# The product with V turned round: channels instead of queries on the partitions

## The chip, the core and the metric

The kernel runs on one core of one Trainium2 chip, in float32 throughout. The metric is the device time of one execution in microseconds (us). The core has five engines that work side by side, each through its own list of instructions in order: TensorE (PE in the profile; PEld is its loading of weights, which overlaps the products), VectorE (DVE), ScalarE (ACT), GpSimd (POOL) and SyncE (SP), which here only issues DMAs. TensorE multiplies a stationary operand (the "weights", loaded first) with a moving one and writes to PSUM, whose banks hold 512 float32 numbers on each of 128 partitions. A product whose output needs only 64 or 32 of the partitions can be one of two or four "column tiles", which stand side by side in the array.

## What is computed

For each of 16 samples: x is 100 x 640, the context 722 x 384, of which the last four rows (`ca`) are tokens of their own.

```python
query = x @ Wq                              # 100 x 640
keyt, valt = enc @ Wk, enc @ Wv             # 718 x 640 each
hs = mha(query, keyt, valt)                 # 8 heads of 80 channels, softmax over 718 keys
ca_q1 = einsum('btc,th->bch', ca, Wq_ca)[:, indices]
ca_q2 = mha(ca_q1, x, x) @ Wq
ca_hs2 = mha(ca_q2, ca @ Wk_ca, ca @ Wv_ca) # softmax over only 4 tokens
out = (hs + ca_hs2) @ Wout + b_out + x
```

## The kernel before, in words

Everything runs in one loop over the samples b = 0 to 15, whose instructions are written out in a fixed order for every engine (a manual schedule: no planner moves anything). One pass of the loop holds, in the order of TensorE's list:

- three groups of scores for b (`scores(b, 0..2, ...)`, L615), each two of the six blocks of 119 or 120 keys, copied by ScalarE to three tiles `st` with keys on partitions and 8 x 100 columns of heads and queries;
- the small products of the token attention (`z_ps`, L821, and `y_ps`, L759);
- before the change, the five transposes (`hst_ps`, L936) of the result of b - 1;
- the values of b and the keys of b + 1 in turn (`Values`, `Keys`, L441 and L472), while VectorE and ScalarE turn the scores into exponentials;
- the last chunk of the keys (`kT_ps`, L566), the projection by Wout of rows that are complete (`project`, L964), and in every second pass the queries of the next two samples (`queries`, L542);
- the product of the exponentials with V (`a_ps`, L1326).

PSUM is divided into three pools of two slots: `ps2` (pairs of banks), `psk` and `ps1` (single banks). The pool `ps1` matters here: both halves of the product with V take its two banks, and so do, next, the third and fourth bank of `scores(b + 1, 1)`, then `z_ps` and `y_ps`. A slot can be written again only when the last reader of its former contents is done.

The product before: the exponentials of 64 or 36 queries (`QC`) are the stationary operand, the 80 channels of one head and a column of ones (`vs`, `D + 1`) the moving one. So queries stand on the partitions of the result, and the sum of the exponentials comes out as an 81st column in the same partition. Four heads (`g`) share a bank. VectorE takes the reciprocals of the four sums, multiplies (L1338, L1340), and adds the tokens' second sums `hs2` (L1347). For the projection the result must have channels on partitions, hence the transposes at the start of the next pass, copied by ScalarE (L949) into `hsT`.

The tokens' second sums: `softmax3` (L866 to L869) makes 8 x 4 weights for each query, `load` (L840) brings the four tokens' values by one DMA of 1 MB on POOL's queue, broadcast to 100 partitions, and `values2` multiplies and adds them on POOL (L883, L890). Also on POOL: the first attention's scores of the tokens (`scores1`, L794 and L801), the sums of the context from which products are saved (`enc_sums`, L507), the masked `m2` (`keys`, L731) and the residual's bias (L921).

SP's list holds the loads of the samples to come (`load_enc`, L229, each waiting until the values of b are done; `load_rest`, `ca`, `load_m`) and the stores of `out` (L986).

The product and the division before (L1326 to L1347):

```python
for g in range(2):
    a_ps = psum1(f"a_ps_{b}_{g}")                 # one bank of ps1 for four heads
    ...
            for lo, hi in QC:                     # two column tiles: 64 and 36 queries
                nc.tensor.matmul(
                    a_v[lo:hi, h % 4],
                    st[i // 2][: KEYS[i], i % 2, h * S + lo : h * S + hi],
                    block(i, h // 4)[: KEYS[i], h % 4],   # 80 channels and the ones
    ...
    nc.vector.reciprocal(rs.unsqueeze(2), a_v[:, :, D : D + 1])
    nc.vector.tensor_tensor(hs[:S, cols]..., a_v[:, :, :D], rs..., ALU.mult)
    if b:
        nc.vector.tensor_tensor(hs[:S, cols], hs[:S, cols], hs2[:, cols], ALU.add)
```

## Time and profile before

| | |
|---|---|
| runs, median (lowest to highest) | 951.72 us (951.39 to 953.53), 3 runs |
| the profiled execution: span from first to last instruction | 950.1 us (no time beside the span is given) |
| TensorE busy | 943.5 us, 99% |
| VectorE / POOL / ScalarE busy | 681.0 / 620.7 / 364.6 us |
| TensorE's share of the chain that ended last | 96% |

In the profile a line such as "L1326 PE MATMUL a_ps<-vs,st" is a group of instructions of one line of the program: engine, operation, the tile written and the tiles read, then shapes (partitions x elements), the count, busy time and mean duration in ns, and after the bar the idle time before them with what ended it. In a timeline the first two numbers are the start from the beginning of the span and the length in us; neighbours of one kind are merged with their count, and one merged row runs a little into the next, since matmuls are pipelined. A float32 matmul shows as two instructions. "to landing" is the time from a DMA's issue until its data is there.

### The profile page before, as it was taken

The numbers are of one execution on the slowest core, as the hardware profiler recorded it, in microseconds if no ns is written. First come the engines' busy times: TensorE is split into PE (matmuls) and PEld (weight loads), VectorE is DVE, ScalarE is ACT, GpSimd is POOL, SyncE is SP. The second block draws the span as 40 slices with busy tenths as digits, with TensorE's granted clock in tenths as the row PEclk, the third lists the DMA queues.
The fourth block names the chain that finished last, engine by engine and source line by source line (L and its number), as shares of the span: only waits on it lengthen the run. The fifth ranks groups of instructions, "written<-read, shape, count | busy, mean of one in ns | idle before, by whom it ended". The sixth has DMA issues, their size and how long they took to land.

```text
span 950.1 us, 22551 instructions
## 1 busy us (share of the span) xinstructions
PE 943.5 (99%) x9679; PEld 798.3 (84%) x9679; DVE 681.0 (72%) x1079; ACT 364.6 (38%) x605; POOL 620.7 (65%) x565
## 2 busy tenths in 40 slices
PE   9999999999999999999999999999999999999998
PEld 6988879788897888888788887987889888897866
DVE  3859794977829687595956959578693886939684
ACT  1244443424335244443524334244431434434241
POOL 5757976876738757594872948657694576748514
PEclk9999999999999999999999999999999999999999
DMA  8822023040310404003040120403113030120200
GB/s 259 290 73 79 2 82 113 1 129 2 94 58 1 116 2 134 4 23 108 1 150 3 42 74 1 137 2 96 35 41 111 1 113 4 54 56 1 93 8 29
DMA packets 45355, 62.28 MB, mean 66 GB/s; under 512 B 13448, under 2 KB 37320, under 8 KB 43656
## 3 DMA queue, kind: packets, MB, share of 16 engines
q1 hardware_dynamic: 41720, 42.97, 15.0%
q0 software_dynamic: 2512, 16.72, 6.0%
q8 instruction: 76, 1.25, 0.5%
q10 hardware_dynamic: 1024, 1.15, 0.4%
q14 instruction: 23, 0.19, 0.1%
HBM read 55.26 MB, written 5.57 MB: 64 GB/s over the span
## 4 chain that ended last, share of the span: by engine, by line
PE 96%; DVE 2%; DMA 1%; issue 0%; ACT 0%; POOL 0%; ACTq 0%; DVEq 0%
PE s_ps L615 13%; PE a_ps L1326 12%; PE v_psA L441 10%; PE v_psB L441 8%; PE kT_ps L566 8%; PE k_psA L472 7%; PE q_ps L542 7%; PE o_ps L964 7%; PE k_psB L472 6%; PE v_psC L441 3%; PE k_psC L472 3%; PE v_ps L382 2%; PE y_ps L759 2%; PE v_psD L441 2%; PE v_psE L441 2%; PE k_psE L472 1%
## 5 line engine op out<-in xcount | busy, mean ns | idle before, releaser
L794 POOL TENSOR_TENSOR e<-ca,g 100x800 f32<-100x800 f32 x64 | 100.0, 1572 | 150.3 <-ACT vs L414 146.5
L883 POOL TENSOR_TENSOR hs<-vb,p 100x640 f32<-100x640 f32 x64 | 105.5, 1657 | 46.7 <-DVE p L869 34.2
L890 POOL TENSOR_TENSOR hs<-hs,hs 100x640 f32<-100x640 f32 x48 | 113.9, 2373 | 3.8
L1326 PEld LDWEIGHTS a_ps<-vs,st 120*36 120x36 f32 (+3 forms) x3072 | 109.1, 125 | 5.6 <-issue 5.5
L1326 PE MATMUL a_ps<-vs,st 120*36 120x81 f32 (+3 forms) x3072 | 111.9, 233 | 0.0
L507 POOL TENSOR_TENSOR enc<-enc 128x240 f32<-128x240 f32 x135 | 98.9, 742 | 19.4 <-DMA enc<-in_enct 12.3
L441 PE MATMUL v_psA<-wv_sb,enc 128*120 128x320 f32 x352 | 109.5, 434 | 0.0
L1153 DVE TENSOR_TENSOR st<-st,over 120x1600 f32<-120x1600 f32 x48 | 106.6, 2222 | 0.0
L650 ACT COPY st<-s_ps 120x800 f32<-120x800 f32 x64 | 49.7, 829 | 148.0 <-PE s_ps L615 148.0
L801 POOL TENSOR_TENSOR e<-e,e 100x800 f32<-100x800 f32 x48 | 90.5, 1885 | 3.8
L441 PE MATMUL v_psB<-wv_sb,enc 128*120 128x320 f32 x296 | 91.9, 433 | 0.0
L615 PE MATMUL s_ps<-qp,kT 64*120 64x100 f32 x1536 | 88.5, 268 | 0.0
L615 PEld LDWEIGHTS s_ps<-qp,kT 64*120 64x120 f32 x1536 | 83.1, 182 | 5.6 <-issue 4.2
L1338 DVE RECIPROCAL rs<-a_ps 100x4 f32<-100x4 f32 x32 | 5.8, 182 | 114.2 <-PE a_ps L1326 114.2
L472 PE MATMUL k_psA<-enc,wk_sb 128*128 128x240 f32 x360 | 87.6, 366 | 0.0
L472 PEld LDWEIGHTS k_psA<-enc,wk_sb 128*128 128x128 f32 x360 | 68.3, 190 | 16.7
L1161 ACT ACTIVATE st<-st 120x1600 f32<-120x1600 f32 x48 | 73.9, 1539 | 22.0 <-DVE st L1153 22.0
L441 PEld LDWEIGHTS v_psA<-wv_sb,enc 128*120 128x120 f32 x352 | 63.2, 183 | 22.6 <-issue 0.5
L1165 DVE TENSOR_TENSOR most<-most,st 120x800 f32<-120x800 f32 x64 | 65.9, 1029 | 20.5 <-ACT st L644 19.1
L472 PE MATMUL k_psB<-enc,wk_sb 128*128 128x240 f32 x300 | 73.0, 366 | 0.0
L441 PEld LDWEIGHTS v_psB<-wv_sb,enc 128*120 128x120 f32 x296 | 54.0, 183 | 21.9 <-DVE vs L412 0.4
L542 PE MATMUL q_ps<-xT,wq_sb 128*128 128x200 f32 x400 | 69.1, 333 | 0.0
(146 smaller groups left out, 1728.2 us busy)
## 6 DMA issues: line engine op xcount, KB each, us to landing
vb<-va_d POOLq DMA_DIRECT2D x16, 1000.0 KB, 7.5
enc<-in_enct SPq DMA_DIRECT2D x30, 240.0 KB, 3.8
enc<-in_enct SPq DMA_DIRECT2D x15, 360.0 KB, 3.3
xT<-in_xt SPq DMA_DIRECT2D x8, 500.0 KB, 4.0
rest<-in_enct SPq DMA_DIRECT2D x31, 120.0 KB, 6.3
xn<-in_x SPq DMA_DIRECT2D x11, 320.0 KB, 4.8
out<-xn SPq DMA_DIRECT2D x11, 320.0 KB, 2.5
ca<-in_cas SPq DMA_DIRECT2D x16, 156.2 KB
```

Source lines behind the costliest of these rows:

```text
L441: nc.tensor.matmul(at[0][j][:KN, : H // 2], a_form(self.enc, f)[:, j * KN : (j + 1) * KN], wv_there.get(f, wv_sb[:, W_AT[f]]), start=first ...
L472: nc.tensor.matmul(at[:, i * KT : (i + 1) * KT], wk_sb[:, W_AT[f], i], a_form(self.enc, f), start=(first and i == 0), stop=last, skip_grou ...
L507: nc.gpsimd.tensor_tensor(out, left, right, op)
L542: nc.tensor.matmul(q_ps[:, : 2 * S].rearrange("p (j s) -> p j s", j=2), wq_sb[:, c, n * P : (n + 1) * P], xT[:, :, c, :], start=(c == 0), ...
L566: nc.tensor.matmul(bank[:, i * KT : (i + 1) * KT], weights[c], a_raw(enc, u, c), start=(i == 0 and c == 0), stop=(c == CC - 1), skip_group ...
L615: nc.tensor.matmul(s_ps[bank][:n, 256 * a + lo : 256 * a + lo + rhs.shape[-1]], kT[rows, c, u, j * KN : (j + 1) * KN], rhs, start=bank not ...
L794: first = nc.gpsimd.tensor_tensor(to, self.ca[:, t, :].unsqueeze(1).to_broadcast([S, NH, S]), g[:, :, t].unsqueeze(2).to_broadcast([S, NH, ...
L801: nc.gpsimd.tensor_tensor(e, e, to, ALU.add)
L883: first = nc.gpsimd.tensor_tensor(to, vb[:S, t, :].rearrange("p (h d) -> p h d", h=NH), p2[:, :, t].unsqueeze(2).to_broadcast([S, NH, D]), ...
L890: nc.gpsimd.tensor_tensor(sums, sums, to, ALU.add)
L1153: return nc.vector.tensor_tensor(st[i], st[i], top.over[:KN].unsqueeze(1).to_broadcast([KN, 2, ROWS]), ALU.subtract,)
L1326: nc.tensor.matmul(a_v[lo:hi, h % 4], st[i // 2][: KEYS[i], i % 2, h * S + lo : h * S + hi], block(i, h // 4)[: KEYS[i], h % 4], start=(i ...
```

## The change

The product with V is turned round: the values are the stationary operand and the exponentials of all 100 queries the moving one, so that channels stand on the partitions and queries along the free axis. Each head's 80 channels are split into 64 "wide" and 16 "narrow" ones. The wide ones of two heads fill two column tiles of 64 in one bank (`a_ps`, four pairs of heads by 100 queries). The narrow ones of a head share a column tile of 32 with 16 columns of ones in another bank (`r_ps`, heads 0 to 3 and 4 to 7 beside each other), so that the sums of the exponentials come out on 16 partitions per head. The narrow products of all heads and keys come first, then the wide ones.

The result now stands as the projection needs it, in another order of channels, to which Wout's rows are loaded (`load_outputs`, 16 DMAs for one). The transposes and ScalarE's copies of them go. The division needs each head's reciprocals on the partitions of its channels: `divide` takes the reciprocal of the narrow bank on VectorE, writes one row per head to DRAM (two DMAs), and reads it back broadcast to 16 partitions for each head and to 64 for pairs (eight and two DMAs), all on SP's queue, into the tile `ratio`. Then VectorE multiplies the narrow bank, adds its two halves (the unwanted part is zeroed by `ratio`), multiplies the wide bank (`scale`), and adds the second sums (`place`).

The tokens' second sums are turned too: the tokens' values `vaT` are computed with channels on partitions and stay there, and the softmax weights of each pass are transposed in blocks of 32 by VectorE, written to DRAM in four DMAs and read back broadcast in ten, on SP's queue; POOL's multiplications and additions then have 500 elements on 128 partitions instead of 640 on 100. `softmax3` and `keys` move to earlier places in the pass.

```diff
-QC = [(0, 64), (64, S)]
+REST = 2 * (D - 64)
+SLOT = D + REST // 2
+VALUES = (0, REST // 2)
+ONES = (D, 0)
+WIDE = (0, REST)
+NARROW = (64, 0)
+FIRST = (0, D - 64)
...
+def load_outputs(load, to, w):
+    rows = w.rearrange("(h k) n -> h k n", h=NH)
+    for h in range(NH):
+        g, e = h // 4, h % 2
+        load(out=to[64 * e : 64 * e + 64, h // 2], in_=rows[h, FIRST[g] : FIRST[g] + 64])
+        at = 32 * (h % 4) + 16 * g
+        load(out=to[at : at + 16, HC - 1], in_=rows[h, 64:] if g == 0 else rows[h, : FIRST[1]])
...
-        def load(self):
-            self.vb = vb = vb_tile(f"vb_{b}")
-            nc.gpsimd.dma_start(out=vb[:S],
-                in_=va_d[b * T : (b + 1) * T, :].unsqueeze(0).to_broadcast([S, T, H]))
...
             nc.vector.reciprocal(sm, sm)
             nc.vector.tensor_tensor(
-                p2, e, sm.unsqueeze(2).to_broadcast([S, NH, T]), ALU.mult
+                p2_in[:S].rearrange("p (h t) -> p h t", h=NH), e, ..., ALU.mult
             )
+            turned = small.tile([P, HT], F32, tag="p2t", name=f"p2t_{b}")
+            nc.vector.transpose(turned, p2_in)
+            p2_d = dram.tile([HT, S], F32, tag="p2_d", name=f"p2_d_{b}", bufs=2)
+            for lo, hi in QZ:
+                nc.sync.dma_start(out=p2_d[:, lo:hi], in_=turned[lo : lo + 32, : hi - lo])
+            heads = p2_d.rearrange("(h t) q -> h (t q)", h=NH)
+            for e in range(2):
+                nc.sync.dma_start(out=self.pb[64 * e : 64 * e + 64, : HC - 1],
+                    in_=heads[e::2].unsqueeze(0).to_broadcast([64, HC - 1, T * S]))
+            for h in range(NH):
+                at = 32 * (h % 4) + 16 * (h // 4)
+                nc.sync.dma_start(out=self.pb[at : at + 16, HC - 1],
+                    in_=heads[h].unsqueeze(0).to_broadcast([16, T * S]))
...
-        def transpose(self, chunks=[(0, HC)], get=psumk):
...
+        def divide(self, rests):
+            b = self.b
+            inverse = small.tile([P, 2, S], F32, tag="inv", name=f"inv_{b}")
+            nc.vector.reciprocal(inverse, rests)
+            inv_d = dram.tile([NH, S], F32, tag="inv_d", name=f"inv_d_{b}", bufs=2)
+            for g in range(2):
+                nc.sync.dma_start(
+                    out=inv_d[4 * g : 4 * g + 4], in_=inverse[16 * (1 - g) :: 32, g])
+            for h in range(NH):
+                at = 32 * (h % 4) + 16 * (h // 4)
+                nc.sync.dma_start(out=ratio[at : at + 16, HC - 1 + h // 4],
+                    in_=inv_d[h].unsqueeze(0).to_broadcast([16, S]))
+            for e in range(2):
+                nc.sync.dma_start(out=ratio[64 * e : 64 * e + 64, : HC - 1],
+                    in_=inv_d[e::2].unsqueeze(0).to_broadcast([64, HC - 1, S]))
+            self.parted = inverse
+            nc.vector.tensor_tensor(inverse, rests, ratio[:, HC - 1 :], ALU.mult)
+
+        def scale(self, wides):
+            for to, cols in self.pieces():
+                nc.vector.tensor_tensor(
+                    to[:, HC - 1], self.parted[:, 0, cols], self.parted[:, 1, cols], ALU.add)
+            for to, cols in self.pieces():
+                nc.vector.tensor_tensor(
+                    to[:, : HC - 1], wides[:, :, cols], ratio[:, : HC - 1, cols], ALU.mult)
+
+        def place(self):
+            for to, cols in self.pieces():
+                nc.vector.tensor_tensor(to, to, self.hs2[:, :, cols], ALU.add)
...
-                for lo, hi in QC:
-                    nc.tensor.matmul(
-                        a_v[lo:hi, h % 4],
-                        st[i // 2][: KEYS[i], i % 2, h * S + lo : h * S + hi],
-                        block(i, h // 4)[: KEYS[i], h % 4],
...
+        rests = psum1(f"r_ps_{b}")[:, : 2 * S].rearrange("p (g q) -> p g q", g=2)
+        for i in range(len(KC)):
+            for g in range(2):
+                for j in range(4):
+                    h = 4 * g + j
+                    nc.tensor.matmul(
+                        rests[32 * j : 32 * j + 32, g],
+                        slot(i, h)[:, NARROW[g] : NARROW[g] + REST],
+                        st[i // 2][: KEYS[i], i % 2, h * S : (h + 1) * S],
...
+        wides = psum1(f"a_ps_{b}")[:, : 4 * S].rearrange("p (c q) -> p c q", c=4)
+        for i in range(len(KC)):
+            for h in range(NH):
+                lo = WIDE[h // 4]
+                nc.tensor.matmul(
+                    wides[64 * (h % 2) : 64 * (h % 2) + 64, h // 2],
+                    slot(i, h)[:, lo : lo + 64],
+                    st[i // 2][: KEYS[i], i % 2, h * S : (h + 1) * S],
...
+        mine.divide(rests)
+        mine.scale(wides)
+        mine.hs2 = now.hs2
+        if b:
+            mine.place()
```

(`pieces` gives the parts of a sample's 100 rows that fall into one block of 128 output rows: one or two, for b = 14 three.)

More of the change, by code (lines that the diff above doesn't have):

```diff
@@ new lines, in pieces @@
+        def pieces(self):
+            b = self.b
+            for r, (lo, n) in enumerate(OC):
+                first, end = max(lo, b * S), min(lo + n, (b + 1) * S)
+                if first >= end:
+                    continue
+                if r not in hsTs:
+                    hsTs[r] = (
+                        spare[0].rearrange("p (c s) -> p c s", c=HC)
+                        if r == len(OC) - 1
+                        else hsT_tile(f"hsT_{r}")
+                    )
+                yield hsTs[r][:, :, first - lo : end - lo], slice(first - b * S, end - b * S)
@@ L1171 @@
             enc_sums(enc)
-            now.load()
             now.softmax1()
@@ L1263 @@
                     nc.scalar.copy(wv_sb[:, W_AT[f]], wv_there.pop(f))
-            second.load()
             if b == 1:
```

233 lines of the change are left out of this document (112 added, 121 removed).

## The prediction

> **What bounds the kernel now.** I read the totals and the chain that ended last first, then the timelines of one steady pass (b = 9, which begins its product with V at 551.28 us), then the DMA rows. The totals and the chain, from the page:
>
> ```profile
> span 950.1 us, 22551 instructions
> PE 943.5 (99%) x9679; PEld 798.3 (84%) x9679; DVE 681.0 (72%) x1079; ACT 364.6 (38%) x605; POOL 620.7 (65%) x565
> PE 96%; DVE 2%; DMA 1%; issue 0%; ACT 0%; POOL 0%; ACTq 0%; DVEq 0%
> ```
>
> TensorE never stands still for long: a microsecond off its own work is a microsecond off the span, and any wait put into its queue is added in full. The other engines have slack. TensorE's timeline around the product (start, duration):
>
> ```profile
> 551.28 6.99 PE L1326 MATMUL a_ps<-vs,st 120*64 120x81 f32 x192
> 558.20 1.93 PE L615 MATMUL s_ps<-qp,kT 64*120 64x100 f32 x32
> ...
> 566.03 0.75 PE L821 MATMUL z_ps<-y,e 100*32 100x33 f32 x64
> 566.71 1.21 PE L759 MATMUL y_ps<-m,xT 128*100 128x96 f32 x10
> 567.75 0.59 PE L936 MATMUL hst_ps<-ident,hs 100*128 100x100 f32 x5
> 568.18 1.26 PE L441 MATMUL v_psA<-wv_sb,enc 128*120 128x320 f32 x4
> ```
>
> Start to start, the product takes 6.92 us, the three groups of scores 7.83 us (558.20 to 566.03, 2.61 each), the transposes of the result 0.43 us (567.75 to 568.18).
>
> **TensorE's own work.** Before, 192 instructions run as pairs of column tiles: 96 pairs of 81 columns, 72 ns a pair, or 0.89 ns a column. After, the wide part has 96 instructions in 48 pairs of 100 columns, the narrow part 96 instructions in 24 fours of 100 columns. At 0.89 ns a column that is 4.27 and 2.14 us. Four column tiles do run side by side: the z row has 64 instructions in 0.68 us, 42.5 ns per four with 33 columns, which is 13 ns above 0.89 a column; with that surcharge the fours cost 2.45. I take 4.35 + 2.25 = 6.6 us, a gain of 0.3 (bounds 0.5 and 0). The five transposes go: 0.43. Over 15 passes: 15 x 0.73 = 11.0 us less; the last pass is summed apart. The other way to write the tokens' values at the start (60 small matmuls for 12) is within a microsecond, and I leave it out.
>
> **The new wait.** Before, a sum is finished on VectorE as soon as its half of the product is there (start, duration, idle before):
>
> ```profile
> 551.45 0.82 DVE L983 TENSOR_TENSOR xn<-o_ps,xn 128x640 f32<-128x640 f32 x1 [0.77 <-PE o_ps L964]
> 554.95 0.18 DVE L1338 RECIPROCAL rs<-a_ps 100x4 f32<-100x4 f32 x1 [2.67 <-PE a_ps L1326]
> 555.16 0.49 DVE L1340 TENSOR_TENSOR hs<-a_ps,rs 100x320 f32<-100x320 f32 x1
> ...
> 558.33 0.18 DVE L1338 RECIPROCAL rs<-a_ps 100x4 f32<-100x4 f32 x1 [1.74 <-PE a_ps L1326]
> 558.54 0.49 DVE L1340 TENSOR_TENSOR hs<-a_ps,rs 100x320 f32<-100x320 f32 x1
> ```
>
> Its two banks are free at 559.03, and the next user of those two banks, the second group of scores, gets to them at 558.20 + 2.61 = 560.8. With channels on partitions the sums of the exponentials lie along the free axis of a few partitions and must be spread over the others. `divide` does that through DRAM: reciprocal, two writes, eight narrow and two wide broadcast reads, all on SP's queue, and VectorE waits in order. Both banks (`r_ps`, `a_ps`) are held until the last product is out, and they are the very two that `scores(b + 1, 1)` takes. In the compiled order, TensorE's third and fourth instruction of that group wait for VectorE. So I time the chain against TensorE, from the product's start.
>
> The rows for its steps: two reciprocals of different width, the issue of a store and of a broadcast load on SP (minimum, median, maximum in ns), and the time to landing (the last column):
>
> ```profile
> L1338 DVE RECIPROCAL rs<-a_ps 100x4 f32<-100x4 f32 x32 | 5.8, 182 | 114.2 <-PE a_ps L1326 114.2
> L830 DVE RECIPROCAL rz<-z_ps 100x8 f32<-100x8 f32 x16 | 3.2, 200 | 0.0
> L1061 SPq DMA_DIRECT2D m_d<-m x5: 319/328/413, 27.1 to 31.1; - x5
> L749 SPq DMA_DIRECT2D ca<-in_cas x15: 314/393/509, 30.3 to 781.7; - x15
> out<-xn SPq DMA_DIRECT2D x11, 320.0 KB, 2.5
> enc<-in_enct SPq DMA_DIRECT2D x4, 60.0 KB, 3.2
> GB/s 0 178 325 213 227 293 179 87 261 79 11 0 0 11 0 0 0 11 0 0 0 0 0 0 0 0 0 0 0 0 11 0 0 0 0 0 0 0 217 347
> ```
>
> 1. The narrow sums end at 2.25; VectorE, free since 552.27, starts at 2.4.
> 2. The reciprocal is now 128x200. Four more elements cost 18 ns, 4.5 each, so 182 + 196 x 4.5 = 1.06 us: 3.5. (Lower bound, if width costs what it costs L1340, (491 - 182) / 316 = 0.98 each: 0.37 us.)
> 3. Two writes at 0.33 each, begun at 3.6 and 3.9. Landing: the 320 KB store took 2.5 us. The last row is the traffic from 541 to 600 us in 40 slices of 1.48; the store ran in the ninth, at 261 GB/s, so without its bytes it would take 1.25. For 1.6 KB I take 2.2, nearer the upper end, because the 60 KB load took 3.2 although it is smaller: the first lands at 5.8, the second at 6.1. In the tenth slice (554.3 to 555.8) the traffic ends, so nothing stands ahead.
> 4. Ten reads at 0.39 (the broadcast load of `ca`) begin at 5.85; the eighth starts at 8.6, the tenth at 9.4. A read lands after 1.25 to 3.2 us (the store's floor, the smallest load, which had other loads beside it); I take 2.4: 11.0 and 11.8.
> 5. VectorE: `rests` times the ratio, 200 from PSUM, by L1340's slope 0.37; one or two adds of 0.2; `wides` times the ratio, 400 from PSUM, 0.57, or 0.75 in two pieces. The add fits before the last landing; so 11.8 + 0.7 = 12.5, and TensorE hears at 12.6.
>
> TensorE itself is there at 6.6 + 2.6 + 0.1 = 9.3. The wait is 3.3 us, and 15 x 3.3 = 49.5 (bounds below). Queued behind it on TensorE is everything. On VectorE the running maximum (562.68 before, 11.4 after the start of the product) waits behind the chain and then the added second sums, to about 13.4; but its second step waits for TensorE's stalled scores anyway, so I count no second wait.
>
> [...]
>
> **The end.** Today's last pass:
>
> ```profile
> 932.87 6.14 PE L1326 MATMUL a_ps<-vs,st 120*64 120x81 f32 x168
> 939.26 1.06 PE L1326 MATMUL a_ps<-vs,st 120*64 120x81 f32 x24
> 941.98 4.50 PE L964 MATMUL o_ps<-wout_sb,spare 128*128 128x320 f32 x16
> 946.51 0.49 DVE L977 TENSOR_TENSOR spare<-o_ps,spare 128x320 f32<-128x320 f32 x1 [1.12 <-PE o_ps L964]
> ```
>
> From 932.9 to 950.1 it takes 17.2 us. After: ratio landed at 11.8, product 0.6 and second sums 0.7 on VectorE, 20 projection matmuls at 4.50 / 16 = 0.27, 5.4, then 0.5 and a store of 0.35 + 2.5: 21.9. That is 4.7 more.
>
> **The tokens' second sums.** The 1 MB load on POOL's queue, known long ahead, becomes four writes and ten broadcast reads on SP's, behind the softmax. What hides it:
>
> ```profile
> 578.43 1.00 DVE L715 STREAM_TRANSPOSE over<-spread 128x800 f32<-128x800 f32 x1
> 580.63 1.88 POOL L801 TENSOR_TENSOR e<-e,e 100x800 f32<-100x800 f32 x1
> 584.79 4.01 POOL L883 TENSOR_TENSOR hs<-vb,p 100x640 f32<-100x640 f32 x2 [2.28 <-DVE p L869]
> 596.31 3.01 POOL L890 TENSOR_TENSOR hs<-hs,hs 100x640 f32<-100x640 f32 x1
> vb<-va_d POOLq DMA_DIRECT2D x16, 1000.0 KB, 7.5
> ```
>
> The weights are now made just ahead of `over`, by 579.3. Four issues (1.3), a landing (2.2) and 7.5 for the megabyte give 590.5; POOL, free at 582.5 and then busy about 3 with the residual's bias and the moved `keys`, waits some 5 us. Its seven steps took 14.5 us (584.79 to 599.32); with 500 elements instead of 640 about 11.4, ending at 602, 2.6 later than before. `place` wants them one pass on, near 620, and the enc sums that follow on POOL wait for loads issued only at 595.9. So nothing. If 18 us of cover were gone, VectorE would stand in `place`, after the banks are free. SP's queue, held to about 585 by these, is free again before the loads of 595.9. VectorE's added work (reciprocal, 0.4 for the turned weights) lies in its idle time; ScalarE only loses the result copies.
>
> **The first pass.** There SP's queue is not empty:
>
> ```profile
> 83.36 0.42 DVE L869 TENSOR_TENSOR p<-e,sm 100x32 f32<-100x32 f32 x1
> 84.55 0.94 SPq L242 DMA_DIRECT2D rest<-in_enct  x2
> 92.41 6.98 PE L1326 MATMUL a_ps<-vs,st 120*64 120x81 f32 x192
> ```
>
> Before, SP had issued everything for pass 0 by 86. Now Wout (16 issues instead of one), the queries' input and the loads of b = 2 stand behind the turned weights of 83.8: their writes have landed at 87.3, and 33 issues (10 + 16 + 7) of 0.39 last to 100.2, with 4.3 MB, 12.4 us at 347 GB/s. The reciprocal's writes, wanted at 92.4 + 3.6 = 96.0, leave 4.2 us late and share the engines with what is in flight; I take 6 more for this pass (bounds 0 and 12).
>
> **The sum.** 950.1 - 11.0 + 49.5 + 6.0 + 4.7 = 999.3 us of span. The page gives no time of the profiled execution beside its span; the median of the runs, 951.72, stands 1.6 above it, which I add: **1001 us**.
>
> **The rivals.** (a) The round trip hides and the change is faster. The chain must be 3.3 us shorter: reciprocal 0.37 (0.7 less), landings at 1.25 both (2.1), issues at 0.31 (0.7), together 3.5. Then the steady waits are gone and the end costs 1.2; with the first pass at 2, 950.1 - 11.0 + 2 + 1.2 = 942.3, and 944 us. With my end and first pass it wins only under a steady wait of (11.0 - 4.7 - 6.0) / 15 = 0.02 us. Each shortening is possible, all three together hardly: 0.08. Between 949.8 and 953.6 (0.2%, about what these times can tell from no change): 0.02.
>
> (b) TensorE restarts slowly after each wait. The first rows of the timeline:
>
> ```profile
> 1.13 2.50 PE L1014 MATMUL idle_ps<-idle 128*128 128x128 f32 x10 [1.13 <-DVE idle L1011]
> ...
> 4.84 2.25 PE L382 MATMUL v_ps<-wv_sb,enc 128*120 128x320 f32 x4
> ...
> 9.42 1.24 PE L382 MATMUL v_ps<-wv_sb,enc 128*120 128x320 f32 x4
> ```
>
> From rest, 128 columns took 250 ns, where 0.89 a column makes 114, and four v_ps took 2.25 us instead of 1.24 later (with load waits in it). The slow stretch lasted from 1.13 to 3.63 or 7.09, 2.5 to 6 us, and half of it was lost. If a wait of 3.3 us does the same, each loses 1.25 to 3 us more; at 1.7, 15 x 1.7 = 25, 1026 us. [...] No steady pass here has a gap to show it. 0.13.
>
> (c) The reads are slow: issues at 0.51 (the row's maximum) and landings of 2.5 and 3.2 add 2.3 us: 16 x 2.3 = 37, 1038 us. 0.10.
>
> (d) Column tiles of 32 do not run four abreast: 96 x 89 ns makes the product 12.8 us and 90 us more; the z row speaks against it. 0.01.
>
> **How the numbers follow.** My own case, a steady wait of 1.3 to 5 us, holds 0.66: 1001 - 30 = 971 to 1001 + 26 = 1027. To hold 8 in 10 I go from 966 to 1036, which takes in (b) and most of (c) and leaves out (a), (d) and the far tails. Faster by over 0.2%: 0.08; within: 0.02; slower: 0.90.
>
> **What would show it.** The waits should list the second group of scores behind VectorE's product with `ratio`, 15 times at 3 to 4 us; SP's rows ten ratio reads a pass at 0.3 to 0.4; the reciprocal near 1.06 us; product instructions at 4.3 and 2.2 us a pass; no hst_ps rows. A TensorE without that wait would prove me wrong.

## The result, and the profile after

| | before | after |
|---|---|---|
| runs, median (lowest to highest) | 951.92 us (951.39 to 953.53), 4 runs | 1103.54 us (1102.45 to 1107.45), 4 runs |
| ratio, 95% interval | | 1.160 (1.158 to 1.162) |
| the profiled execution | span 950.1 us | 1107.45 us, span 1105.7 us |

The change costs 152 us. The forecast, 1001 us (966 to 1036), had the direction and the main place of the loss, and a third of its size.

The page of the changed kernel: totals, the granted clock by slices, and the chain that ended last.

```profile
span 1105.7 us, 23133 instructions
PE 1000.2 (90%) x9647; PEld 837.1 (76%) x9647; DVE 689.3 (62%) x1116; ACT 356.7 (32%) x578; POOL 552.8 (50%) x554
PEclk9899599898998989899998989989899998989898
PE 60%; DVE 19%; DMA 9%; SPq 8%; issue 3%; ACT 0%; DVEq 0%; POOL 0%
```

TensorE now stands still for a tenth of the span, and although it has less to do than before its busy time rose from 943.5 to 1000.2 us: part of its work runs at a lower clock (0.931 of full in the mean of the span, 0.999 before). The round trip of the reciprocals (DVE, DMA, SPq) has come into the chain. Around one steady product, the one of b = 8 by the count of starts (the one at 551.28 us before, which the prediction called b = 9), TensorE's timeline, start and duration first:

```profile
642.11 2.27 PE L1382 MATMUL r_ps<-st,vs 120*32 120x100 f32 x96
644.32 4.34 PE L1394 MATMUL a_ps<-st,vs 120*64 120x100 f32 x96
648.59 1.93 PE L647 MATMUL s_ps<-qp,kT 64*120 64x100 f32 x32
650.45 1.28 PE L647 MATMUL s_ps<-qz,kT 32*120 32x200 f32 x20
653.21 0.57 PE L647 MATMUL s_ps<-qz,kT 32*120 32x200 f32 x2 [1.48 <-DVE inv L993]
656.11 1.66 PE L647 MATMUL s_ps<-qz,kT 32*120 32x200 f32 x10 [2.34 <-DVE hsT L1015]
657.69 5.63 PE L647 MATMUL s_ps<-qp,kT 64*120 64x100 f32 x64
```

The product is 6.48 us from start to start (6.92 before). Then come two waits for the two banks, 1.48 and 2.34 us, and behind them 64 score instructions take 5.63 us for which 3.60 were enough before:

```profile
561.62 3.60 PE L615 MATMUL s_ps<-qp,kT 64*120 64x100 f32 x64
```

The changed kernel's stretch by windows (length; busy time and count of PE, PEld, DVE, ACT and POOL; PEclk, DMA share, GB/s):

```profile
651.60:655.20 3.60, 0.69 (x4) 0.28 (x2) 0.70 (x3) 1.44 (x2) 0.00 (x0) 1.00 0.43 83
655.20:662.00 6.80, 5.89 (x52) 5.43 (x54) 2.29 (x5) 1.24 (x3) 0.00 (x0) 0.50 0.02 4
662.00:664.20 2.20, 2.20 (x48) 1.86 (x48) 1.60 (x2) 0.53 (x2) 0.00 (x0) 1.00 0.00 0
```

The granted clock falls to 0.50 at 655.2, near the end of the second wait, and is back at full at 662.0, 6.8 us later. The other steady stretches are alike: the clock is low for 6.8 us in ten of the fourteen and for 10.2 us in four. VectorE's timeline and then SP's show the chain, and last stand the rows of the read issues (minimum, median, maximum in ns):

```profile
644.46 1.41 DVE L975 RECIPROCAL inv<-r_ps 128x200 f32<-128x200 f32 x1 [1.34 <-PE r_ps L1382]
652.69 0.36 DVE L993 TENSOR_TENSOR inv<-r_ps,ratio 128x200 f32<-128x200 f32 x1 [6.83 <-DMA ratio<-inv_d]
655.32 0.64 DVE L1015 TENSOR_TENSOR hsT<-a_ps,ratio 128x384 f32<-128x384 f32 x2 [1.90 <-DMA ratio<-inv_d]
```

```profile
645.89 1.13 SPq L978 DMA_DIRECT2D inv_d<-inv  x2
647.58 3.85 SPq L983 DMA_DIRECT2D ratio<-inv_d  x8
651.47 1.30 SPq L988 DMA_DIRECT2D ratio<-inv_d  x2
```

```profile
L983 SPq DMA_DIRECT2D ratio<-inv_d x128: 302/418/1877, 125.1 to 1088.8; - x128
L988 SPq DMA_DIRECT2D ratio<-inv_d x32: 608/629/1268, 128.7 to 1090.0; - x32
```

The waits of the whole span (total, times, longest):

```profile
PE s_ps L647 <- DVE inv L993: 45.6, 15, 16.3
PE s_ps L647 <- DVE hsT L1015: 26.0, 13, 2.4
PE y_ps L791 <- POOL m L763: 9.8, 1, 9.8
PE o_ps L1033 <- DVE spare L1021: 8.8, 1, 8.8
...
ACT beside L1165 <- DMA wvca<-in_wvca: 17.5, 1, 17.5
...
POOL ratio L1197 <- DMA m_d<-ratio: 9.5, 1, 9.5
```

Cut at the starts of the 16 products, each span falls into four parts: the start (up to the first product), the first stretch (to the product of b = 1), the 14 stretches that follow (the "passes 1 to 14" of the expectations), and the end (from the last product's start). The table holds them for every kernel, from TensorE's timelines; the runs are told below.

| us | start | first stretch | 14 stretches (each against before) | end | span | median of the runs |
|---|---|---|---|---|---|---|
| before | 92.4 | 58.3 | 782.2 | 17.2 | 950.1 | 951.9 |
| after | 104.5 | 81.8 | 892.9 (+7.9) | 26.5 | 1105.7 | 1103.5 |
| e1_no_trip | 104.2 | 62.3 | 776.9 (-0.4) | 18.4 | 961.8 | 964.5 |
| e2_dummies | 101.5 | 81.3 | 890.5 (+7.7) | 25.4 | 1098.6 | 1102.2 |
| e2b_four_dummies | 102.6 | 81.3 | 849.1 (+4.8) | 26.0 | 1059.0 | 1061.8 |
| e3_startup | 101.1 | 83.0 | 891.2 (+7.8) | 26.0 | 1101.4 | 1101.3 |
| e3b_memset_later | 100.6 | 82.4 | 887.0 (+7.5) | 26.0 | 1096.0 | 1099.9 |
| e4_wout_first | 101.9 | 70.8 | 889.4 (+7.7) | 26.1 | 1088.2 | 1091.1 |
| e5_scalar_empties | 103.1 | 77.2 | 820.4 (+2.7) | 25.5 | 1026.2 | 1026.8 |
| v1_pool_scales | 93.0 | 59.2 | 784.5 (+0.2) | 26.6 | 963.3 | 965.1 |
| e6_start_and_wout | 92.5 | 71.5 | 890.2 (+7.7) | 26.0 | 1080.2 | 1080.8 |
| v3_picked_end | 92.7 | 60.6 | 784.5 (+0.2) | 19.0 | 956.8 | 959.1 |
| v4_softmax_back | 92.9 | 60.1 | 774.7 (-0.5) | 19.1 | 946.8 | 948.2 |
| e7_two_queues | 101.0 | 80.6 | 879.6 (+7.0) | 25.4 | 1086.5 | 1088.6 |

So the 155.6 us of span are 12.1 at the start, 23.5 in the first stretch, 110.7 in the fourteen, and 9.3 at the end. The first of these moves by 3 to 4 us between kernels that do not touch it (101.0 to 104.5); less than that is not read from it.

### The profile page after: what moved, and what is told of

Read it like the earlier page. It is cut to its first block, busy times and chain, and to the rows that moved or that the text cites. A ratio compares the mean times of both kernels' runs of the same rounds, so it can differ in the third digit from the quotient of the medians.

```text
span 1105.7 us, 23133 instructions
## 1 busy us (share of the span) xinstructions
PE 1000.2 (90%) x9647; PEld 837.1 (76%) x9647; DVE 689.3 (62%) x1116; ACT 356.7 (32%) x578; POOL 552.8 (50%) x554
## 3 DMA queue, kind: packets, MB, share of 16 engines
q8 instruction: 76, 1.25, 0.5%
## 4 chain that ended last, share of the span: by engine, by line
PE 60%; DVE 19%; DMA 9%; SPq 8%; issue 3%; ACT 0%; DVEq 0%; POOL 0%
PE s_ps L647 12%; PE kT_ps L598 6%; PE q_ps L574 6%; PE o_ps L1033 6%; SPq L983 6%; DMA ratio<-inv_d 4%; PE v_psB L473 4%; PE v_psA L473 4%; PE k_psA L504 3%; PE k_psB L504 3%; PE r_ps L1382 3%; PE v_psC L473 3%; DVE most L1241 3%; DMA inv_d<-inv 3%; DVE vs L444 2%
## 5 line engine op out<-in xcount | busy, mean ns | idle before, releaser
L647 PE MATMUL s_ps<-qz,kT 32*120 32x200 f32 x768 | 70.4, 398 | 76.0 <-DVE inv L993 45.6
L929 POOL TENSOR_TENSOR hs<-pb,vaT 128x500 f32<-128x500 f32 x64 | 79.9, 1259 | 113.2 <-DMA pb<-p_d 92.2
L647 PEld LDWEIGHTS s_ps<-qp,kT 64*120 64x120 f32 x1536 | 117.1, 244 | 9.5 <-issue 7.7
L647 PE MATMUL s_ps<-qp,kT 64*120 64x100 f32 x1536 | 122.5, 332 | 0.0
L539 POOL TENSOR_TENSOR enc<-enc 128x240 f32<-128x240 f32 x135 | 101.2, 759 | 37.0 <-DMA enc<-in_enct 29.7
L647 PEld LDWEIGHTS s_ps<-qz,kT 32*120 32x120 f32 x768 | 47.3, 201 | 88.6 <-issue 76.2
L1229 DVE TENSOR_TENSOR st<-st,over 120x1600 f32<-120x1600 f32 x48 | 96.0, 2002 | 0.0
L993 DVE TENSOR_TENSOR inv<-r_ps,ratio 128x200 f32<-128x200 f32 x16 | 5.9, 366 | 129.7 <-DMA ratio<-inv_d 129.7
L676 ACT COPY st<-s_ps 120x400 f32<-120x400 f32 x64 | 28.3, 499 | 135.4 <-PE s_ps L647 135.4
L1394 PE MATMUL a_ps<-st,vs 120*64 120x100 f32 (+1 forms) x1536 | 69.5, 250 | 0.0
```

What stands on the lines that cost most here:

```text
L539: nc.gpsimd.tensor_tensor(out, left, right, op)
L647: nc.tensor.matmul(s_ps[bank][:n, 256 * a + lo : 256 * a + lo + rhs.shape[-1]], kT[rows, c, u, j * KN : (j + 1) * KN], rhs, start=bank not ...
L929: first = nc.gpsimd.tensor_tensor(to, pb[:, :, t], va.to_broadcast([P, HC, S]), ALU.mult)
L1229: return nc.vector.tensor_tensor(st[i], st[i], top.over[:KN].unsqueeze(1).to_broadcast([KN, 2, ROWS]), ALU.subtract,)
L1394: nc.tensor.matmul(wides[64 * (h % 2) : 64 * (h % 2) + 64, h // 2], slot(i, h)[:, lo : lo + 64], st[i // 2][: KEYS[i], i % 2, h * S : (h + ...
```

## The experiments

**Without the round trip** (e1_no_trip). The two writes and ten reads of `divide` are taken out, so the kernel leaves the division undone.

> The changed kernel without the round trip: the reciprocal is still taken, but its two writes to DRAM and the ten reads into `ratio` are left out, so the sums are multiplied by whatever `ratio` holds and the division is left out of the result. Theory 1 (the second scores wait for the two banks until the round trip is over, and TensorE's clock then falls for some microseconds): both go with the trip. Per pass 1 to 14 the changed kernel is 7.9 us behind the kernel before; with the trip gone it should be 0.9 us ahead of it (product -0.44, transposes -0.43). Pass 0 loses its 18.3 us of wait and about 4 us of slow clock, and ends within 1 us of before's. The end loses its 8.8 us wait and about 2.3 us of slow clock. The start-up keeps its +12.1. Sum: 950 + 12 - 13 + 1 - 2 = 948 of span, so about 950 us by the clock of the runs; the bounds are 943 and 956. Rival (what is slow is something the change does beside the trip: narrow tiles, the turned second sums on GpSimd, VectorE's larger product): the time stays above 1000 us, and the passes stay several us longer than before's although TensorE's wait for `inv` is gone.

Measured: 964.5 us, ratio to before 1.013 (1.011 to 1.016). The fourteen stretches fall from +7.9 to -0.4, so the trip carries the steady loss and the turned products and sums none. That is half of the 0.87 a stretch that the product and the transposes save. Most of the rest goes at one place, where k_psE waits for VectorE to empty the V bank: in the stretch of b = 8 everything ahead of it keeps the 0.87, and what stands behind it has lost 0.45 to 0.49 us of that, though the list of waits has only 0.22 there. The time is 14 us above the 950 expected, and outside its bounds: 13 were subtracted for the fourteen stretches where 5.3 came, the first stretch is at +4.0 and not +1, the end at +1.2 and not -2. What is left without the trip is 11.8 at the start, 4.0 in the first stretch and 1.2 at the end; the division is not the whole loss. In the first stretch TensorE's timeline has a wait for the queries' input, whose load stood behind Wout's:

```profile
121.45 1.29 PE L791 MATMUL y_ps<-m,xT 128*100 128x96 f32 x10 [1.94 <-DMA xT<-in_xt]
122.53 2.38 PE L473 MATMUL v_psA<-wv_there,enc 128*120 128x320 f32 x4
```

Four instructions take 2.38 us after that one wait, not the 1.26 of the prediction's row; the granted clock was 0.50 from 122.5 to 124.7 us.

**Keeping TensorE at work during the wait** (e2_dummies, then e2b_four_dummies).

```diff
+        if g == 1 and b:
+            for _ in range(9):           # e2b: 4
+                nc.tensor.matmul(s_ps[0], ident, wq_sb[:, :4, :P], start=True, stop=True, ...)
         for part, last in zip((rests, halves) if g == 1 else ...
```

> The changed kernel with nine more matmuls of 128x128 by 128x512 in each pass but the first, just ahead of the second scores group, into its first bank, which the scores then open anew, so that nobody reads them. They take about 0.43 us each (a 320-column matmul takes 0.27 to 0.28 us from start to start), 3.9 us in all, and need nothing of the round trip: they fill the gap of 1.5 + 2.3 us in which TensorE waits for the two banks. The wait is not shortened by it, TensorE is only kept at work. Theory 1a (after the gap the clock has fallen to about half and is back only some 6 us later, which costs 3.5 to 4 us in every pass): granted clock in the second scores back to 0.9 and more, scores after the gap in 4.4 to 5.2 us and not 8.0, so each of 15 passes is 3.5 us shorter and the time falls to about 1053 us (1045 to 1062) although each pass has more work. Rival 1b (the scores after the gap are slow for a reason of their own, such as the banks, their operands or traffic on the ports): more work, nothing gained, 1103 us or up to 1110. Rival 1c (the matmuls do not fit into the gap): up to 59 us slower, 1160 us.

Measured: 1102.2 us, the same as without them. That decides nothing, since the matmuls were twice as long as assumed: a float32 matmul is two instructions, 18 of 0.444 us are 8.0 us a stretch. But e1's stretches plus 8.0 are -0.4 + 8.0 = +7.6, and +7.7 was measured, with the granted clock at 0.988 over the span. So in the steady stretches the waits for the banks and the slowness had gone, and just the dummies' own time had come. Four of them fit the gap:

> As the run with nine extra matmuls, but with four. In that run each extra matmul of 512 columns turned out to be two instructions of 0.444 us, so nine took 8.0 us and not 3.9; its passes were all alike (62.09, 65.17, 70.55 us), which is what the kernel without the round trip takes plus 8.0, with no wait left and the clock at 0.99. Four take 3.55 us, just under the gap of 1.5 + 2.3. Theory 1a (the clock falls in the gap, and its return costs 3.5 to 4 us in each pass): a pass is that without the trip (54.0, 57.0, 62.4) plus about 3.8 of gap or dummies, 57.8 instead of 62.3, so 14 passes gain about 4.4 each and the time falls to about 1042 us (1033 to 1055). Rival 1b (the scores after the gap are slow for a reason of their own, not because TensorE stood still): passes stay at 62 to 62.5 and the time at 1100 to 1105 us.

Measured: 1061.8 us, 42 less than the changed kernel, though each stretch has more work in it. TensorE's timeline of the product of b = 8, and the window behind the wait:

```profile
625.89 3.70 PE L673 MATMUL s_ps<-wq_sb,ident 128*128 128x512 f32 x8
629.52 0.61 PE L647 MATMUL s_ps<-qz,kT 32*120 32x200 f32 x6
631.23 0.90 PE L647 MATMUL s_ps<-qz,kT 32*120 32x200 f32 x10 [1.09 <-DVE hsT L1025]
632.06 3.60 PE L647 MATMUL s_ps<-qp,kT 64*120 64x100 f32 x64
```

```profile
630.50:634.50 4.00, 3.27 (x56) 3.06 (x58) 2.23 (x5) 0.85 (x3) 0.00 (x0) 1.00 0.03 6
```

The same scores behind the same chain take 3.60 us again, at clock 1.00. Theory 1a holds and 1b falls: they are slow because TensorE had stood still. The forecast of 1042 was 20 us too good, since the gap costs more than its two waits; the 32 score instructions that it splits into three pieces, for one, take 2.3 us where they took 1.56 in one piece in e1. From the table: after minus e2b, (892.9 - 849.1) / 14 = 3.1 us a stretch, is the slow clock; e2b minus e1, (849.1 - 776.9) / 14 = 5.2, is the gap, dummies and remaining wait together. The changed kernel's own clock agrees: in the fourteen stretches TensorE worked 6.5 us each at 0.50, of which half, 3.25 us, is lost.

**Wout before the division** (e4_wout_first).

```diff
-            if b == 0:
-                load_outputs(nc.sync.dma_start, wout_sb, wout)     # in loads()
...
         if b == 0:
+            load_outputs(nc.sync.dma_start, wout_sb, wout)
             enc_sums(enc)
```

> The changed kernel with the sixteen loads of Wout issued at the start of pass 0, where SP's queue is idle from 65 to 96 us, and not after the exponentials of that pass. Theory 3 (in pass 0 the two writes of the reciprocals stand behind 16 issues of Wout on SP's queue: the reciprocal is done at 112.2 us, its writes are issued at 120.4): the writes go out at 112 to 113 us, TensorE's wait in the second scores of pass 1 falls from 16.3 + 2.0 to about 8 + 2 us, and the time falls by 8 to about 1095 us (1092 to 1098); the clock is low after the shorter wait too. Rival (the queue is held by the broadcast reads of the second sums' probabilities, issued from 98.8 to 105.5 us, or by the loads of the next images behind Wout): the writes go out at 116 us or later and under 4 us are gained.

Measured: 1091.1 us, a microsecond below the forecast's range; the first stretch falls from 81.8 to 70.8. SP's timeline of the changed kernel's first stretch shows what stood ahead of the writes:

```profile
105.57 0.52 SPq L89 DMA_DIRECT2D wout_sb<-in_wout  x1
...
115.85 0.58 SPq L94 DMA_DIRECT2D wout_sb<-in_wout  x1
...
120.42 1.25 SPq L978 DMA_DIRECT2D inv_d<-inv  x2
```

and that of e4:

```profile
109.79 1.12 SPq L978 DMA_DIRECT2D inv_d<-inv  x2
```

**The start** (e3_startup, e3b_memset_later; both together in e6_start_and_wout). The loop's order is written out, but ahead of the loop a planner orders the instructions.

```diff
-    nc.gpsimd.memset(ratio[:, HC - 1 :], 0.0)          # e3, e3b: into the first pass
...
+    with tc.issue_after(w_copied.ins):                  # e3: behind the last copy of Wk
         for g in range(2):
             nc.scalar.copy(narrow...)
...
         if b == 0:
+            nc.gpsimd.memset(ratio[:, HC - 1 :], 0.0)   # e3
             enc_sums(enc)
+            nc.gpsimd.memset(ratio[:, HC - 1 :], 0.0)   # e3b, in its place
```

> The changed kernel with two instructions of the start moved: the memset of the last two columns of `ratio` goes from the part that the planner orders to the first lines of pass 0 on GpSimd, and the two copies into `narrow` on ScalarE may be issued only after the last copy of Wk's transposes. Theory 2 (the planner put the memset, which waits 9.55 us for the store of m out of the same room, ahead of the masked m2, so that TensorE waits 9.75 us in y_ps and then runs at a low clock, and put the narrow copies, which wait 17.5 us for Wvca, ahead of the copies of Wk): the first product of V begins at 92 to 93 us of the span as before and not at 104.5, and the time falls by 12 to about 1091.5 us (1089 to 1095). Rival (the start is late for its DMA loads or for the 30 matmuls of the turned va, and the list only shows it): the first product begins at 100 us or later and at most 4 us are gained, 1099 us or more.

> The changed kernel with the memset of the last two columns of `ratio` behind the thirteen sums of the second image's encoder input on GpSimd, which wait for that image (until 66 us). As the first line of pass 0 it had still been listed ahead of the masked m2 of the second key group, waited there 7.51 us for the store of m, and TensorE waited 7.72 us. Theory 2: with the memset out of the way y_ps goes on at once, as before, the transposes of Wk run at full clock (1.82 us for 13 and not 2.98), the first product of V begins at 92.5 to 94 us and the time falls by 8 to 12 us from the changed kernel's, to 1092 to 1096 us. Rival (the copies into `narrow`, which stay where they are here and wait 17.5 us for Wvca on ScalarE, ahead of the copies of Wk, hold the start as well): the first product begins at 99 us or later, and at most 5 us are gained.

Measured: 1101.3 and 1099.9 us, starts of 101.1 and 100.6: both forecasts missed. The waits on TensorE of e3 and then of e3b say why:

```profile
PE y_ps L791 <- POOL m L763: 7.7, 1, 7.7
```

```profile
PE w_ps L1141 <- ACT wk_sb L1144: 4.9, 1, 4.9
```

In e3 the memset, though moved, was still listed ahead of masked m2 parts and still waited for the store; in e3b it was out of the way, and the copies into `narrow`, which wait for Wvca, held the copies of Wk, as that run's rival had it. Two holds stand side by side, each enough for most of the loss. e6 takes both away, with Wout moved as in e4:

> The changed kernel with both instructions of the start moved (the memset of `ratio` behind the sums of the encoder input, the copies into `narrow` behind those of Wk) and Wout's loads at the start of pass 0; the division as in the change. Each of the two moves alone had left the start at 100.6 to 101.1 us, since the other still held it; in the run in which ScalarE and GpSimd empty and scale, both together gave 93.0. Theory 2 (two holds, each enough by itself) and theory 3 (Wout ahead of the reciprocals' writes): first product at 93 us, pass 0 at 71 us, the rest as in the changed kernel (passes 1 to 14 at +7.9 and the end at +9.3): 950 + 0.6 + 12.5 + 110.7 + 9.3 = 1083 of span, about 1083 to 1086 us. Rival: the start of 93 us came from the other edits of that run, and the first product begins at 99 us or later, 1090 us or more.

Measured: 1080.8 us, 2 us under the forecast; start 92.5, first stretch 71.5. Theory 2 is right with both holds named; each move alone showed almost nothing, and Wout's move alone left the start at 101.9 (e4).

**The banks or VectorE?** (e5_scalar_empties).

```diff
+            for to, cols in self.pieces():
+                nc.scalar.copy(to[:, : HC - 1], wides[:, :, cols])
+            nc.scalar.copy(inverse, rests)      # once the writes have read it
             self.parted = inverse
-            nc.vector.tensor_tensor(inverse, rests, ratio[:, HC - 1 :], ALU.mult)
+            nc.vector.tensor_tensor(inverse, inverse, ratio[:, HC - 1 :], ALU.mult)
```

and `scale` multiplies the wide tiles in place.

> The changed kernel with the two banks emptied by ScalarE: it copies the wide tiles unscaled into their place and the rests over the reciprocals once these are written out; VectorE does the same multiplications as before in SBUF, at the same place of its list, so it still stands still for the round trip in every pass. Theory 1 (what stops TensorE is that the two banks are held): TensorE does not wait any more, its clock stays up, and passes 1 to 14 fall from +7.9 to between 0 and +1.5 over the kernel before; pass 0 keeps its wait, since there the writes of the reciprocals are late on SP's queue, and the end keeps its +9. Time about 1000 us (990 to 1012). Rival 4 (VectorE, 62% busy, standing still for 8.7 us in order, is what delays the pass: maxima, subtractions and the emptying of the V and K banks come late): TensorE's wait moves to `vs` and `kT` on VectorE, the passes stay at +5 or more, and the time at 1060 us or more.

Measured: 1026.8 us, between the two theories and nearer to the first. The wait for the banks has left the fourteen stretches, and +7.9 becomes +2.7. What remains is rival 4; from the waits on TensorE:

```profile
PE k_psE L504 <- DVE vs L444: 26.1, 14, 3.6
...
PE v_psD L473 <- DVE z L864: 11.0, 12, 4.2
```

Of these 37.1 us, 3.6 lie in the first stretch; the other 33.5, 2.4 a stretch, are waits for a VectorE that still stands for the trip in order. The clock, low in four of the fourteen stretches, adds 0.6 a stretch. So the trip blocks twice: by the banks, and behind those by VectorE's list. The second block is hidden in the changed kernel, where k_psE waits 5.1 us in all.

**Taking both blocks away** (v1_pool_scales, v3_picked_end, v4_softmax_back).

```diff
+        def engine(self):
+            return nc.vector if self.split else nc.gpsimd   # last image: VectorE
...                                      # scale, place and the product with ratio:
-                nc.vector.tensor_tensor(...)
+                self.engine().tensor_tensor(...)
```

with e5's copies, both moves of e6 at the start, and Wout early.

> ScalarE empties the two banks, and the scaling and the sum with the tokens' part go to GpSimd, which waits in every pass for the next scores anyway (L826: 309.9 us in 14 waits); VectorE keeps only the reciprocal, and the division of the last image. With it the memset of `ratio` behind the sums of the encoder input, the copies into `narrow` behind those of Wk, and Wout's loads at the start of pass 0. Theories 1, 2 and 3 together: start as before (+0.5), pass 0 +3 (xT of the next images late), passes 1 to 14 at -0.4 each as in the run without the trip (-5.7), end +9.3 as in the changed kernel, since the last division still goes over DRAM: 950.1 + 7 = 957 of span, about 959 us (950 to 966). [...]

Measured: 965.1 us. Start 93.0, first stretch +0.9, end +9.4 as forecast; the fourteen are at +0.2, not -0.4, since TensorE waits for VectorE again, though little, and for the last division:

```profile
PE k_psE L504 <- DVE vs L444: 10.1, 14, 1.0
PE o_ps L1039 <- DVE spare L1027: 9.1, 1, 9.1
```

For the second, v3 spreads the last reciprocals by matmuls:

```diff
+                    nc.tensor.matmul(spread[:, c * S : (c + 1) * S],
+                        pick[:, at], inverse[:, g], ...)    # pick: 0 and 1, made from ident
```

> As the run in which GpSimd scales, and for the last image no trip over DRAM: VectorE's reciprocals are spread over the partitions by six matmuls with weights of zeros and ones (12 instructions of 0.09 us, 1.05 us on TensorE behind the last product), and VectorE multiplies by them out of a bank. That run's end took 26.6 us from the start of the last product, 9.1 of them a wait for the division, and its last projection then took 7.64 us at a low clock in place of 5.6. Forecast: the scaled tile is there 9.2 us after the product starts and not 15.5, the projection takes 5.6 us, the end 18 us, and the time is 8.5 less than that run's 965.1, 956.5 us (954 to 959). Rival (the last projection waits for the tokens' second sums on GpSimd, which end 8.3 us after the product starts, and the clock falls all the same): 960 us or more.

Measured: 959.1 us, just above the range; the end is 19.0 us where 26.6 were, one more than forecast. The twelve instructions took from 944.24 to about 945.8, 1.58 us and not 1.05. For the first, v4 puts `softmax3` back:

> As the run before it, with the tokens' second softmax at its place of the kernel before on VectorE (behind the fourth V and K blocks, not ahead of the last step of the maxima). In the run in which GpSimd scales, TensorE waited 14 times, 10.1 us in all, in k_psE for VectorE to empty the V bank; the softmax (0.85 us) stands ahead of that emptying, where before it stood behind. Forecast: the wait goes, 0.7 us of each of 14 passes, and 946.5 us (944 to 950) is under the kernel before (951.8). Rival (VectorE is late there because GpSimd's scaling slows the maxima, 2.71 and 2.46 us in place of 2.0, or the second sums now come late on GpSimd and hold the sums of the encoder input): at most 0.2 us per pass is gained, 953 us or more.

Measured: 948.2 us (946.2 to 949.6), ratio to before 0.996 (0.995 to 0.997): under the kernel before by 3.5 us, as forecast. The engines' row of its page, and TensorE's timeline of its end:

```profile
PE 934.4 (99%) x9659; PEld 784.8 (83%) x9659; DVE 665.2 (70%) x1020; ACT 368.5 (39%) x623; POOL 626.1 (66%) x656
```

```profile
934.19 1.58 PE L986 MATMUL spread<-inv,spare 128*128 128x100 f32 x12
937.48 5.62 PE L1075 MATMUL o_ps<-wout_sb,spare 128*128 128x320 f32 x20 [1.71 <-DVE spare L1063]
```

TensorE is back at 99%, with 9.1 us less to do than before: 11.0 was the prediction's figure for fifteen passes. The fourteen stretches gain 0.53 each of the 0.87 that the product and the transposes give. Why not more was not looked for.

**A shorter trip** (e7_two_queues): the eight narrow reads go from `nc.sync` to `nc.scalar`.

> The changed kernel with the eight narrow reads of the reciprocals on ScalarE's queue, so that the two wide reads follow the writes on SP at once. In the changed kernel SP issues eight narrow reads of 0.42 us and then two wide ones of 0.63, and VectorE waits 6.8 us for the narrow and then 1.9 us for the wide. Theory 1, with the length of the trip as its measure: the narrow ones land when they did, the wide ones some 3 us earlier, so VectorE's second wait and TensorE's second wait (25.9 us in 13) go; with them about 2 us of gap, and 0.5 to 1 us of slow clock, in each of 14 passes: 1103 - 38 = 1065 us (1058 to 1078). Against it stands that ScalarE stands in its list until the writes have landed and then issues for 3.4 us, ahead of the copies of the first scores, which VectorE's maxima wait for. Rival 6 (the wide reads take their place among the DMA queues and land no earlier, or the copies of the scores come so late that the gain is lost): 1095 us or more.

Measured: 1088.6 us, between the two forecasts. TensorE's second wait all but went, from 2.0 us a stretch to 0.2, as theory 1 has it; but its first grew from 2.1 to 3.1 us, so it waits only 0.85 us less for the banks, and 7.0 of the 7.9 stayed. Why the narrow reads landed later was not tested. TensorE's timeline and windows of the product at 633.19 us:

```profile
644.86 0.57 PE L647 MATMUL s_ps<-qz,kT 32*120 32x200 f32 x2 [2.06 <-DVE inv L993]
645.78 0.90 PE L647 MATMUL s_ps<-qz,kT 32*120 32x200 f32 x10 [0.35 <-DVE hsT L1015]
646.61 5.23 PE L647 MATMUL s_ps<-qp,kT 64*120 64x100 f32 x64
```

```profile
642.80:646.90 4.10, 1.69 (x18) 1.19 (x18) 2.50 (x8) 1.50 (x2) 0.00 (x0) 1.00 0.03 7
646.90:650.30 3.40, 3.40 (x39) 3.40 (x36) 0.40 (x1) 0.86 (x2) 0.00 (x0) 0.50 0.01 2
650.30:652.00 1.70, 1.70 (x33) 1.60 (x34) 0.75 (x1) 0.91 (x3) 0.00 (x0) 1.00 0.00 0
```

This is one of the three best stretches of e7: after a gap of 2.06 + 0.35 us the clock is low for 3.4 us. In the other eleven it is low for 6.8 or 10.2 us, as in the changed kernel, and over the fourteen TensorE worked 6.2 us a stretch at 0.50, against 6.5 there. So a wait shorter by 0.85 us brings back itself, 0.95 in all, and almost nothing of the clock; where dummies filled the gap it stayed at 1.00 (e2b, the window from 630.50).

## Why the prediction was wrong, step by step

- **TensorE's own work: right.** Narrow 2.21, wide 4.27 us from start to start (forecast 2.25 and 4.35), and no hst_ps rows. Beside it, "within a microsecond, and I leave it out" for the start was the first step that failed: +12.1 us. The arithmetic of the 60 small matmuls was harmless. The planner's lists ahead of the loop were not: the memset behind a store out of the same room, and the copies behind Wvca. Both stood in the compiled order on GpSimd and ScalarE, and the prediction weighed no list of the start.
- **The new wait: right in kind, 0.5 short in its own terms.** The reciprocal took 1.41 us, not 1.06: (1408 - 182) / 196 = 6.3 ns an element, above both slopes used. The ten reads cost 0.42 and 0.63 to issue, not 0.39; the wide one, over 64 partitions, was priced like a small load. The write landed in about 1.1 us (second issue at 646.45, first read out at 647.58), not 2.2; the last read took about 3.2 (issued at 652.1, VectorE at 655.32), not 2.4. Their sum is 4.3, where 4.6 was taken. The banks came free 14.0 us after the product's start, not 12.6, and TensorE waited 1.48 + 2.34 = 3.8, not 3.3 (4.1 as a mean of the fourteen). The gap as a whole, by e2b against e1, cost 5.2.
- **Rival (b), given 0.13 and 1.7 us a wait, came about at 3.1 us.** This is the step with the largest error in the steady part: 892.9 - 849.1 = 44 us over the fourteen. The prediction left the term out of its sum; the low chance was its author's estimate, with no steady wait of that length in the kernel before to show it. In the 3.6 us before the clock fell, TensorE still worked 0.69 us (the window from 651.60), and two waits of 1.48 and 2.34 us, or of 2.06 and 0.35 (e7), were followed by a clock of 0.50. The price was too low as well: 1.7 us was an estimate between the bounds of 1.25 and 3. It is what a low stretch of 3.4 us costs (half of it, as in the stretch of e7), and the clock of the changed kernel stayed low for 6.8 or 10.2.
- **"I count no second wait": true of the time, not of the mechanism.** With the banks emptied by ScalarE, VectorE's standing still left a stretch 2.7 us above the kernel before (e5). In the changed kernel it lay behind the wait for the banks.
- **The first pass: 6 taken, bounds 0 to 12; 23.5 measured.** The issues from Wout to the last load took 14.8 us (105.57 to 120.33), 0.6 to 0.7 each where 0.39 was taken, and the reciprocal itself was late, 6.3 us after the product's start, because VectorE was at the first softmax. The clock's share came on top: it was 0.50 for 23.9 us (115.87 to 139.76), in which TensorE worked 7.4. Of the 23.5, 11.1 go with Wout's place alone (e4) and 19.5 with the trip alone (e1), so they overlap; v1, which has Wout early and one wait of 1.4 us left for the banks, is at +0.9.
- **The end: 4.7 forecast, 9.3 measured.** The ratio landed 13.9 us after the product's start (11.8), and the projection took 7.77 us, not 5.4, at a granted clock of 0.50 in its first half.
- **The tokens' second sums: nothing, as forecast.** GpSimd waits for `pb` 14 times, 92.2 us in all, and no TensorE wait follows from it; e1 has the turned sums whole, and its fourteen stretches are no longer than those of the kernel before.

Counted up, the forecast had 49 us of span and missed 106: 12 at the start, 15 in the first stretch, 5 at the end, and 75 in the fourteen, of which 44 are the slow clock and 31 the gap and the half of TensorE's gain that did not arrive. The clock alone would have put the time out of the range (1001 + 44); it is the term that was mis-sized most.

## What to carry to other kernels

A wait put into the list of a TensorE that is 99% busy had three prices here: the wait itself (3.8 us in the stretch shown), the slow clock after it (3.1 us a stretch), and the delay of what the engine that waits for the trip does next (2.4 us a stretch in e5). A shorter wait brought back little more than what it was shortened by (e7: 0.95 us for 0.85). What brought back nearly all of the steady loss was to empty the bank first and let an idle engine finish the division (v1: +0.2 us a stretch for +7.9). When a change reuses a room or adds a copy near the start, read the planner's lists there too, and when two holds may stand side by side, take both away before judging either. Count what else a queue issues in the pass where it is fullest, at the price of its slowest rows.

## What the runs showed of the hardware

- In the changed kernel's trace the granted clock was 0.50 for 6.83 us in ten of the fourteen steady stretches, for 10.24 in four and for 23.89 in the first pass; these lengths, and those at 1.00 between them (54.61 to 64.85 us in the steady stretches), are whole multiples of 3.41 us. In e7 it was low for 3.4, 6.8 or 10.2 us. It could fall after the wait and not in it: in the stretch of e7 shown above at 646.9 us, 1.1 us behind the second wait.
- The length of a wait alone did not decide whether the clock fell. In e1 the last wait of 2.94 us left it at 1.00, and the 20 projection instructions behind it took 5.62 us; one of 1.94 us was followed by 0.50 (first pass of e1), and so was one of 1.59 us in e2b (at 999.9 us: 64 score instructions behind it took 5.23 us, not 3.60). Of e5's thirteen waits of 1.72 or 1.73 us, three brought it down (the four k_psE instructions behind them took 1.48 to 1.84 us) and ten did not (1.08). What else decides was not tested.
- SP's issue of a DMA differed with its shape: 0.54 us for the strided 1.6 KB write, 0.42 for a read to 16 partitions, 0.63 for one to 64 (medians of the changed kernel).
- While GpSimd scaled (v1, b = 8: 565.7 to 571.8 us), the two pairs of VectorE's running maxima (tile `most`) that ran at the same time took 2.71 and 2.46 us; in the kernel before and in the changed one, with GpSimd idle, they took 2.02 and 2.01. So work given to GpSimd was not free to VectorE.
